# A four-layer graph network on one core: where the edge sums of layer 2 are made

## The chip, the cores and the metric

The kernel runs on one core of one Trainium2 chip. The metric is the device time of one execution in microseconds (us). The time before the change is the median of 3 runs. The profile comes from one more execution, recorded by the hardware profiler. The engines are TensorE (PE in the profile, its weight loads PEld), VectorE (DVE), ScalarE (ACT), GpSimd (POOL) and SyncE (SP). SP does nothing but issue DMA transfers in this kernel; ACT and POOL issue some as well.

## The reference, cut to what matters

There are 4096 nodes with 256 features each. `adj` is a 4096 x 4096 matrix of zeros and ones with ones on its diagonal, used by all four layers. Each layer adds its output to its input and normalizes the rows.

```python
# layer 0
agg = adj @ x / max(rowsum(adj), 1);  y = relu(concat(x, agg) @ W + b)
# layer 1, two steps n = 0, 1
R = (adj + I) / rowsum(adj + I)
A = top-p softmax of (Xa W1' W2') (Xa W3')', rows cut to mass 0.9 and renormalized
Xf = R @ Xf;  Xa = A @ Xa;  Z += Xf @ U1[n].T + Xa @ U2[n].T
# layer 2: the edge features are adj itself
nn = adj @ x
ne = einsum('ij,ji->i', adj, adj)            # the edge sums
y  = concat(x, nn, ne) @ weight + bias
# layer 3
y  = relu(normalized(adj + I) @ x @ W + b)
```

The edge sum of node i is the sum over j of adj[i, j] * adj[j, i]. It depends on `adj` alone, so it can be computed at any time before the end of layer 2.

## The kernel before

The nodes are cut into 32 tiles of 128 (`NT = 32`, `P = 128`). The host lays `adj` out twice in blocks of 128 x 128: `adjt` holds the transposed blocks that TensorE needs as weights, `adjn` the blocks of the other orientation. Both are float32 in DRAM, 2 MB for each tile of rows.

**Layer 0** runs over the 32 tiles. POOL loads `adjt` with a cast from float32 to uint8 (two DMAs per tile, L249); SP stores the bytes to the DRAM tensors `adj8_d`, which all later stages read. ScalarE casts each piece of eight blocks to the float32r format that TensorE takes (L252). The line L167 is the product of a tile row of `adj` with all node rows, each kept as an upper and a lower half, 256 + 256 columns.

**Layer 1, step 0.** While the attention logits of one tile are computed, an earlier tile is reduced to its 16 largest entries (`KEPT`), whose rows of x are gathered by POOL (`gather`, L642) and multiplied on TensorE (L733). VectorE finds maxima and their columns (`groups` L403, `tops` L498 to L502), chooses how many to keep (`pick`), and `flag` writes rows that need more work to a list in DRAM (L576, an indirect DMA of POOL). The loop of `run_step` gives each tile eight groups g of 512 columns. A group of `pieces` issues two logit products (L384), a part of the attention product, and `neighbours`: a cast of four blocks to `adjq` (L653) and four products into `acc_r` for R @ Xf (L656). In step 0 `neighbours` also makes the edge sums: POOL loads half a tile of `adjn` with a cast to uint8 (L662), ScalarE casts four blocks to float32r (L665), and TensorE multiplies the blocks of both orientations into the PSUM tile `nef_ps` (L668):

```python
for j in range(GP):
    jt = g * GP + j
    nc.tensor.matmul(pn[:, :P], a[:, j, :], b[:, j, :], start=(jt == 0),
                     stop=(jt == NT - 1))
```

In `r_end` VectorE multiplies the 128 x 128 result with the identity and sums along the rows into the column `nef[:, i]` (L682). Because `nef_ps` holds a PSUM bank, `acc_r` uses one bank in step 0 and takes turns between two banks only afterwards (`nef_done`). In `mix` the results are multiplied with U1 and U2 (L794), added up on VectorE (L796), and a key product follows (L802). The products of the first four tiles of R @ Xf run ahead of the first attention tile.

**Layer 1, step 1** has the same loop; its attention tiles are dense (L741), and its rows' normalization takes a power on POOL (`rstd`, L191). POOL has little else there: the scatter of `flag` and some gathers for tiles that were put off.

**Layer 2** runs `main` for each tile: four pieces of bytes (`a8`, five buffers, loaded by SP from `adj8_d`, L1077), ScalarE's casts (L1079), 32 products (L167) into the PSUM tile `acc`, which takes turns between two banks. `l2_end` of the tile before follows: ScalarE copies one half of `acc` (L1101), VectorE adds the other (L1102), adds the edge sum times its weight row (L1110) and the prepared rest `u` (L1111), and normalizes (L185 to L196) into `x3`, which SP stores (L1114). `l2_y` of the tile before that transposes `x3` on TensorE (L177) and multiplies it with the weights of layer 3 (L1121); VectorE splits the result into halves `yh`. The rows `x2i` and `u` are loaded by SP (L1104, L1106) and added on VectorE (L1107, L1108). **Layer 3** repeats `main` with `yh`.

Each engine runs its instructions in one fixed order. That order is not the one of the source: the framework's planner interleaves the instructions of neighbouring tiles.

Of the kernel before, what the change touches and what calls it, by code (L numbers as in the profile page):

```python
# [48 lines left out]
def gnn_stack(ctx, tc, x, adjt, adjn, w0, b0, w1, w2t, w3t, u1t, u2t, ln_g, ln_b, w2, b2, w3, b3, out):  # L49
# [12 lines left out]

    const = ctx.enter_context(tc.tile_pool(name="const", bufs=1))
# [50 lines left out]
    adj8_d = [dram.tile([P, NT, P], U8, name=f"adj8_{it}_d") for it in range(NT)]  # L114
    h_d = dram.tile([N + P, D], F32, name="h_d")
# [209 lines left out]
    with tc.tile_pool(name="l1", bufs=1, reuse_waits="tile") as l1:  # L325

        cur = {"late": False, "n": 0, "nef_done": False}
# [224 lines left out]
        def flag(st):  # L552


            pb = half("mm")
            later = st.get("later")
            if later is None:
                nc.tensor.matmul(pb[:1, 0:1], st["bad"], ones_col, start=True, stop=True)
                st["nb"] = small("nbad", 1, I32)[:1, :]
                nc.scalar.copy(st["nb"], pb[:1, :1])  # L560
                return
            nc.tensor.matmul(pb[:, 0:1], ones_sq, st["bad"], start=True, stop=True)
            nc.tensor.matmul(pb[:, 1:2], before, st["bad"], start=True, stop=True)
            sofar, slot = small("sofar"), small("slot")
            nc.vector.tensor_add(sofar, later["base"], pb[:, 0:1])

            i = st["tile"]
            at, rows_i = slots_of[cur["n"]][:, i : i + 1], ids[:, i : i + 1]
            nc.vector.scalar_tensor_tensor(slot, pb[:, 1:2], later["base"], spare, op0=ALU.add, op1=ALU.subtract)
            nc.vector.scalar_tensor_tensor(at, slot, st["bad"], spare, op0=ALU.mult, op1=ALU.add)  # L570
            later["base"] = sofar
            if i == NT - 1:

                st["to"] = to = small("to_last", 1, I32, 1)
                nc.vector.scalar_tensor_tensor(to, st["bad"], float(P), rows_i, op0=ALU.mult, op1=ALU.add)
            nc.gpsimd.indirect_dma_start(  # L576
                out=list_d[cur["n"]], out_offset=bass.IndirectOffsetOnAxis(ap=at, axis=0), in_=rows_i, in_offset=None)

# [68 lines left out]
        def neighbours(n, i, g, acc_r, pn, xf):  # L647
# [11 lines left out]
            if pn is not None:  # L659
                if g % (NLC // 2) == 0:  # L660
                    cur["b8"] = cur["w"].tile([P, NT // 2, P], U8, tag="adjn8", name="adjn8", bufs=2)
                    nc.gpsimd.dma_start(cur["b8"], adjn[i, :, g * GP : g * GP + NT // 2, :])  # L662
                b = cur["w"].tile([P, GP, P], F32R, tag="adjn", name="adjn", bufs=2)
                k = g % (NLC // 2) * GP
                nc.scalar.copy(b, cur["b8"][:, k : k + GP, :])  # L665
                for j in range(GP):
                    jt = g * GP + j
                    nc.tensor.matmul(pn[:, :P], a[:, j, :], b[:, j, :], start=(jt == 0),  # L668
                                     stop=(jt == NT - 1))

        def r_acc(i):

            return ps_acc.tile([P, 512], F32, tag=("acc", "nef")[i % 2 if cur["nef_done"] else 0], name="acc_r", bufs=1)

        def r_end(i, acc_r, pn):
# [3 lines left out]
            if pn is not None:  # L679

                junk = spare_row.bitcast(F32)[:, :P]
                nc.vector.scalar_tensor_tensor(junk, pn[:, :P], 1.0, ident, op0=ALU.mult, op1=ALU.mult,  # L682
                                               accum_out=nef[:, i : i + 1])
            nc.sync.dma_start(rows(xf_d, i), xf_new)

        def r_product(n, i, xf):

            acc_r, pn = r_acc(i), None
            if n == 0:
                pn = ps_acc.tile([P, 512], F32, tag="nef", name="nef_ps", bufs=1)  # L690
            for g in range(NLC):
                neighbours(n, i, g, acc_r, pn, xf)
            r_end(i, acc_r, pn)

        def pieces(n, st, nxt, ops, rs_now=()):
# [10 lines left out]
            if with_r:  # L706
                i, = rs_now
                acc_r, pn = r_acc(i), None
                if n == 0:
                    pn = ps_acc.tile([P, 512], F32, tag="nef", name="nef_ps", bufs=1)  # L710
# [12 lines left out]
            for g in range(NLC):  # L723
# [19 lines left out]
                if with_r:  # L743
                    neighbours(n, i, g, acc_r, pn, cur["xf"])
                for f in ops.get(g, ()):
                    f()
            if st is None:
                for i in rs_now:
                    r_product(n, i, cur["xf"])
# [6 lines left out]
            if with_r:  # L756
                r_end(i, acc_r, pn)
# [158 lines left out]
        def run_step(n, es):  # L916
# [99 lines left out]
            if n == 0:  # L1016
# [7 lines left out]
                cur["nef_done"] = True  # L1024
                for i in range(FIRST[1][0][0]):
                    r_product(1, i, cur["next"])
# [47 lines left out]
    with tc.tile_pool(name="l23", bufs=1, reuse_waits="tile") as l23:  # L1074
        def piece(it, c):
# [3 lines left out]
            nc.scalar.copy(a, a8)  # L1079
            return a  # L1080

        ahead = [piece(0, c) for c in range(NJP)]
        zh = load_halves(l23.tile([P, 4 * J0 * D], F32, name="scratch"), zu_d[:N, :], nc.sync, slice(0, D))
# [14 lines left out]

        def l2_end(it, acc):
# [7 lines left out]
            nc.vector.tensor_add(xi, xi, b2_sb)  # L1107
            nc.vector.tensor_add(u, u, xi)  # L1108
# [8 lines left out]
        def l2_y(it, x3):  # L1117
# [4 lines left out]
            y = l23.tile([P, 1, D], F32, tag="y", name="y", bufs=2)  # L1122
# [20 lines left out]
        for it in range(NT):  # L1143
            acc = main(it, lambda jt: zh[:, jt, :])
            if it > 1:
# [53 lines left out]
```

## Time and profile before

| | us |
|---|---|
| median of 3 runs (3349.98 to 3359.43) | 3354.87 |
| the profiled execution: its time | 3313.77 |
| its span, first to last instruction | 3312.0 |
| TensorE busy | 3017.6 (91%) |
| VectorE busy | 2393.5 (72%) |
| ScalarE busy | 1873.9 (57%) |
| POOL busy | 782.7 (24%) |
| edge products L668, busy | 149.4 |
| edge casts L665, busy | 159.1 |

The profiled execution took 1.2% less than the median of the runs. Busy times are sums of durations, and the durations of TensorE overlap those of their neighbours, since matmuls are pipelined; what a matmul holds up is read from start to start of neighbouring rows. In rows of the order of time, the columns are the start, the duration, the engine, the line, the operation, output and inputs, the shape, and how many instructions were merged; brackets hold the idle time ahead and what ended it. In rows of groups, the last parts are busy time and mean duration in ns of one, then the idle time ahead of the group and its releasers.

### The profile page before, as it was taken

What the parts mean: (1) busy time and instruction counts of PE and PEld (TensorE: products, weight loads), DVE (VectorE), ACT (ScalarE), POOL (GpSimd) and SP (SyncE); (2) the same over time, 40 slices, a digit from 0 to 9 for tenths busy, and PEclk for the clock granted to TensorE, in tenths of its full rate; (3) what the DMA queues carried; (4) which work ended last, traced back from release to release, by engine and by line L of the source; (5) the groups of instructions that cost most, each with busy time, mean ns of one, the idle gap of its engine ahead of it and who ended that gap; (6) DMA issues with size and microseconds to landing.
All of it is one profiled execution on the core that took longest, in us unless ns stands there. A gap on an engine that the chain in (4) does not pass through costs nothing. (4 is left out here: it accounts for less than half of the span.)

```text
span 3312.0 us, 46373 instructions
## 1 busy us (share of the span) xinstructions
PE 3017.6 (91%) x14600; PEld 2465.7 (74%) x14600; DVE 2393.5 (72%) x7121; ACT 1873.9 (57%) x3162; POOL 782.7 (24%) x916
## 2 busy tenths in 40 slices
PE   6999888999999997879989898989999787999998
PEld 5888667888888885658877777777788545888886
DVE  6888858878777776357988897888799673444444
ACT  3555666777777774455555454545455333666664
POOL 1111146666666665100000001000100001000000
PEclk9999989999999998889999999999999898999999
DMA  9988367787777776140000111011011133333332
GB/s 175 143 134 139 68 105 130 135 138 137 136 137 137 136 137 143 56 134 30 25 23 23 32 38 31 26 32 39 24 38 30 42 131 126 110 109 107 102 108 81
DMA packets 247906, 300.30 MB, mean 91 GB/s; under 512 B 34688, under 2 KB 201536, under 8 KB 247648
## 3 DMA queue, kind: packets, MB, share of 16 engines
q0 software_dynamic: 46624, 105.07, 22.8%
q1 hardware_dynamic: 188800, 180.93, 18.8%
q10 hardware_dynamic: 12224, 11.23, 1.1%
q8 instruction: 118, 1.93, 0.3%
q14 instruction: 140, 1.15, 0.1%
HBM read 331.17 MB, written 66.58 MB: 120 GB/s over the span
## 5 line engine op out<-in xcount | busy, mean ns | idle before, releaser
L656 PE MATMUL acc_r<-xh,adjq 128*128 128x512 f32 x2048 | 617.5, 433 | 22.4 <-ACT adjq L653 17.7
L741 PE MATMUL acc_bank<-xa,at 128*128 128x256 f32 x2304 | 568.8, 388 | 31.0 <-ACT at L719 30.5
L642 POOL DMA_INDIRECT G<-x_d,cols x512 | 499.4, 975 | 302.2 <-PE acc_bank L733 163.0
L167 PE MATMUL acc<-xh,a 128*128 128x512 f32 x2048 | 516.5, 405 | 17.8 <-DVE xh L144 14.0
L741 PEld LDWEIGHTS acc_bank<-xa,at 128*128 128x128 f32 x2304 | 425.3, 194 | 92.1 <-ACT at L719 41.3
L653 ACT CAST adjq<-adj 128x512 fp32r<-128x512 uint8 x512 | 316.0, 619 | 295.1 <-PE acc_r L656 97.8
L656 PEld LDWEIGHTS acc_r<-xh,adjq 128*128 128x128 f32 x2048 | 382.7, 193 | 117.6 <-ACT adjq L653 42.2
L167 PEld LDWEIGHTS acc<-xh,a 128*128 128x128 f32 x2048 | 384.6, 191 | 103.0 <-ACT xh L143 17.0
L403 DVE MAX8 cand<-e 128x8 f32<-128x256 f32 x1024 | 381.1, 414 | 93.1 <-ACT e L385 92.0
L191 POOL TENSOR_TENSOR rstd<-ve,mhalf 128x1 f32<-128x1 f32 x168 | 102.7, 611 | 1378.7 <-DVE ve L189 1338.9
L385 ACT COPY e<-lg 128x512 f32<-128x512 f32 x552 | 318.9, 584 | 176.9 <-PE lg L384 176.0
L384 PE MATMUL lg<-kS,q 128*128 128x512 f32 x1104 | 392.2, 440 | 10.7 <-ACT e L385 10.4
L1079 ACT CAST a<-a 128x1024 fp32r<-128x1024 uint8 x256 | 267.7, 1048 | 150.4 <-PE acc L167 121.7
L733 PE MATMUL acc_bank<-G,dg 128*128 128x256 f32 x1024 | 277.8, 392 | 51.5 <-DMA G<-x_d,cols 40.6
L500 DVE FIND_INDEX8 cols<-top,e 128x8 uint32<-128x4096 f32 x64 | 282.8, 4419 | 0.0
L733 PEld LDWEIGHTS acc_bank<-G,dg 128*128 128x128 f32 x1024 | 194.7, 194 | 100.7 <-DMA G<-x_d,cols 49.0
L719 ACT COPY at<-at_ps 128x512 f32<-128x512 f32 x296 | 173.5, 588 | 113.1 <-PE at_ps L716 111.6
L167 PE MATMUL acc<-yh,a 128*128 128x512 f32 x1024 | 233.7, 390 | 0.0
L252 ACT CAST a<-a 128x1024 fp32r<-128x1024 uint8 x128 | 133.5, 1048 | 157.4 <-PE acc L167 121.3
L167 PEld LDWEIGHTS acc<-yh,a 128*128 128x128 f32 x1024 | 192.2, 188 | 39.6
L384 PEld LDWEIGHTS lg<-kS,q 128*128 128x128 f32 x1104 | 182.9, 192 | 32.5 <-ACT e L385 19.4
L716 PE MATMUL at_ps<-ident,e 128*128 128x128 f32 x1184 | 183.5, 279 | 22.0 <-issue 13.8
(281 smaller groups left out, 4637.2 us busy)
## 6 DMA issues: line engine op xcount, KB each, us to landing
adj<-adj_d SPq DMA_DIRECT2D x256, 128.0 KB
a<-adj_d SPq DMA_DIRECT2D x256, 128.0 KB
a<-in_adjt POOLq DMA_DIRECT2D x64, 256.0 KB
adj_d<-a SPq DMA_DIRECT2D x64, 256.0 KB
adjn<-in_adjn POOLq DMA_DIRECT2D x64, 256.0 KB
x_d<-x SPq DMA_DIRECT2D x65, 128.0 KB
G<-x_d,cols POOLq DMA_INDIRECT x512
xf_d<-xf_new SPq DMA_DIRECT2D x64, 128.0 KB
```

The lines of the kernel that those rows point to most:

```text
L167: nc.tensor.matmul(acc, a[:, j, :], halves(jt), start=(jt == 0), stop=(jt == NT - 1))
L384: nc.tensor.matmul(pl[:, :LC], q[k], kS[:, s], start=(k == 0), stop=(k == 1))
L385: nc.scalar.copy(l[:, s], pl[:, :LC])
L403: nc.vector.max(dst[:, 8 * g : 8 * g + 8], src[:, g * GW : (g + 1) * GW])
L500: nc.vector.max_index(st["at"][:, 8 * r : 8 * r + 8], t8, st["e"][:, :N])
L642: nc.gpsimd.indirect_dma_start(out=g, out_offset=None, in_=x1_d, in_offset=bass.IndirectOffsetOnAxis(ap=st["at"][:, k : k + 1], axis=0))
L653: nc.scalar.copy(a, cur["a8"][:, g % 2 * GP : (g % 2 + 1) * GP, :])
L656: nc.tensor.matmul(acc_r, a[:, j, :], xf[:, jt, :], start=(jt == 0), stop=False)
L716: nc.tensor.transpose(ps[:, j, :], e[:, (g * G + j) * P : (g * G + j + 1) * P], ident)
L733: nc.tensor.matmul(acc_a, dg[:, k % 4, :], st["G"][k], start=(k == 0), stop=(k == KEPT - 1))
L741: nc.tensor.matmul(acc_a, ats[g][:, j, :], cur["xa"][:, jt, :], start=(jt == 0), stop=(jt == NT - 1))
L1079: nc.scalar.copy(a, a8)
```

## The change

The edge sums leave step 0. `neighbours`, `r_product` and `r_end` lose the loads, casts, products and the final multiply-and-sum, and `acc_r` takes turns between two banks in both steps. A second set of DRAM tensors, `adjn8_d`, receives `adjn` cast to uint8: in step 1, four DMAs on POOL behind each tile's list scatter, DRAM to DRAM, 512 KB read and 128 KB written by each. In layer 2 the new function `edge_sums` loads a tile's 512 KB of `adjn8_d` into a quarter of the scratch buffer (which until then holds the pieces that `zh` is split from), takes the bitwise and with the four `a8` pieces of the same tile as 32-bit integers, sums over the 32 blocks as uint16 (each holds two byte sums side by side), casts the bytes to float32, and sums over the partitions with a product of one column of ones on TensorE. The pieces `a8` therefore stay in use until VectorE has read them. The additions of `x2i` and `u` move from VectorE to POOL, and `y` has one buffer instead of two.

```diff
+    adjn8_d = [dram.tile([P, NT, P], U8, name=f"adjn8_{it}_d") for it in range(NT)]
...
-            nc.gpsimd.indirect_dma_start(
+            put = nc.gpsimd.indirect_dma_start(
                 out=list_d[cur["n"]], out_offset=bass.IndirectOffsetOnAxis(ap=at, axis=0), in_=rows_i, in_offset=None)
+            if cur["n"] > 0:
+
+                with tc.issue_after(put.ins):
+                    for c in range(NJP):
+                        s = slice(c * JP, (c + 1) * JP)
+                        nc.gpsimd.dma_start(adjn8_d[i][:, s, :], adjn[i, :, s, :])
...
-            if pn is not None:
-                if g % (NLC // 2) == 0:
-                    cur["b8"] = cur["w"].tile([P, NT // 2, P], U8, tag="adjn8", name="adjn8", bufs=2)
-                    nc.gpsimd.dma_start(cur["b8"], adjn[i, :, g * GP : g * GP + NT // 2, :])
-                b = cur["w"].tile([P, GP, P], F32R, tag="adjn", name="adjn", bufs=2)
-                k = g % (NLC // 2) * GP
-                nc.scalar.copy(b, cur["b8"][:, k : k + GP, :])
-                for j in range(GP):
-                    jt = g * GP + j
-                    nc.tensor.matmul(pn[:, :P], a[:, j, :], b[:, j, :], start=(jt == 0),
-                                     stop=(jt == NT - 1))
-
         def r_acc(i):
-
-            return ps_acc.tile([P, 512], F32, tag=("acc", "nef")[i % 2 if cur["nef_done"] else 0], name="acc_r", bufs=1)
...
+            return ps_acc.tile([P, 512], F32, tag=("acc", "nef")[i % 2], name="acc_r", bufs=1)
...
-            if pn is not None:
-
-                junk = spare_row.bitcast(F32)[:, :P]
-                nc.vector.scalar_tensor_tensor(junk, pn[:, :P], 1.0, ident, op0=ALU.mult, op1=ALU.mult,
-                                               accum_out=nef[:, i : i + 1])
...
             nc.scalar.copy(a, a8)
+            bytes_of.append(a8)
             return a
...
+        def edge_sums(it, a8s):
+
+
+            k = it % 4 * J0 * D
+            n32 = scratch[:, k : k + NT * P // 4].bitcast(I32)
+            nc.sync.dma_start(n32.bitcast(U8).rearrange("p (j i) -> p j i", i=P), adjn8_d[it])
+            W = JP * P // 4
+            for c, a8 in enumerate(a8s):
+                s = slice(c * W, (c + 1) * W)
+                nc.vector.tensor_tensor(n32[:, s], n32[:, s], a8.rearrange("p j i -> p (j i)").bitcast(I32), op=ALU.bitwise_and)
+            two = l23.tile([P, P // 2], U16, tag="two", name="two", bufs=2)
+            with nc.allow_low_precision("sums of up to 32 * 257, exact"):
+                nc.vector.tensor_reduce(two, n32.bitcast(U16).rearrange("p (j i) -> p i j", i=P // 2), axis=AX.X, op=ALU.add)
+            sums = l23.tile([P, P], F32, tag="sums", name="sums", bufs=2)
+            nc.vector.tensor_copy(sums, two.bitcast(U8))
+            ps = half("acc")
+            nc.tensor.matmul(ps[:, 0:1], sums, ones_col, start=True, stop=True)
+            nc.vector.tensor_copy(nef[:, it : it + 1], ps[:, 0:1])
...
-            nc.vector.tensor_add(xi, xi, b2_sb)
-            nc.vector.tensor_add(u, u, xi)
+            nc.gpsimd.tensor_tensor(xi, xi, b2_sb, op=ALU.add)
+            nc.gpsimd.tensor_tensor(u, u, xi, op=ALU.add)
...
-            y = l23.tile([P, 1, D], F32, tag="y", name="y", bufs=2)
+            y = l23.tile([P, 1, D], F32, tag="y", name="y", bufs=1)
...
         for it in range(NT):
             acc = main(it, lambda jt: zh[:, jt, :])
+            edge_sums(it, bytes_of[it * NJP : (it + 1) * NJP])
```

## The prediction

> **What bounds the kernel now.** I read the stages first (busy time of each engine in stretches of the span; columns PE, PEld, DVE, ACT, POOL, then granted clock, DMA share, GB/s), since the change takes work from step 0 (460 to 1274 us), adds transfers to step 1 (1440 to 2784) and VectorE work to layer 2 (2784 to 3064).
>
> ```profile
> 460.00:1274.00 814.00, 761.39 (x4005) 647.44 (x4004) 641.59 (x1875) 566.12 (x1118) 524.75 (x561) 0.99 0.75 134
> 1440.00:2784.00 1344.00, 1217.11 (x5894) 974.51 (x5893) 1080.73 (x3483) 672.91 (x1140) 108.69 (x127) 0.96 0.15 40
> 2792.00:3064.00 272.00, 269.36 (x1198) 216.15 (x1197) 123.86 (x351) 177.55 (x254) 17.01 (x31) 1.00 0.37 114
> ```
>
> TensorE bounds step 0 (94%) and layer 2 (99%); VectorE is at 79% in step 0, at 46% in layer 2. POOL and DMA have room in step 1. The chain of waits says the same of its last 560 us: TensorE's L167 alone.
>
> Then TensorE's order of time in step 0:
>
> ```profile
> 828.43 1.02 PE L733 MATMUL acc_bank<-G,dg 128*128 128x256 f32 x4
> 829.11 1.28 PE L656 MATMUL acc_r<-xh,adjq 128*128 128x512 f32 x4
> 830.23 0.56 PE L668 MATMUL nef_ps<-adjn,adjq 128*128 128x128 f32 x4
> 830.62 0.66 PE L364 MATMUL mm_bank<-xt,wq_sb 128*128 128x128 f32 x4
> ...
> 838.55 0.70 PE L733 MATMUL acc_bank<-G,dg 128*128 128x256 f32 x2 [0.74 <-DMA G<-x_d,cols]
> ...
> 845.77 0.71 PE L802 MATMUL mm_bank<-w3t_sb,xt 128*128 128x128 f32 x4 [0.58 <-DVE z L424]
> ```
>
> Ends overlap, so costs are start to start: four edge products (L668) hold TensorE from 830.23 to 830.62, 0.40 us. A tile takes 27.3 us (the flag product L562 starts at 824.59, then at 851.90). Two idles matter: one for a gather G, one for VectorE, which is late at L796 after its 4.42 us searches (L500).
>
> The removed groups and the rows that price additions:
>
> ```profile
> L665 ACT CAST adjn<-adjn 128x512 fp32r<-128x512 uint8 x256 | 159.1, 621 | 2.3 <-DMA adjn<-in_adjn 2.3
> L668 PE MATMUL nef_ps<-adjn,adjq 128*128 128x128 f32 x1024 | 149.4, 265 | 0.0
> L441 DVE TENSOR_REDUCE m_l<-e 128x1 f32<-128x4096 f32 x4 | 17.7, 4419 | 25.2 <-ACT e L385 25.2
> L435 DVE TENSOR_REDUCE m<-cand 128x1 f32<-128x128 f32 x64 | 18.1, 283 | 4.4 <-DVEq L618 2.9
> L1111 DVE TENSOR_TENSOR t<-t,u 128x256 f32<-128x256 f32 x32 | 13.6, 425 | 1.1
> ```
>
> Last, VectorE in a layer 2 tile:
>
> ```profile
> 2902.08 0.42 DVE L1102 TENSOR_TENSOR agg<-agg,acc 128x256 f32<-128x256 f32 x1 [1.64 <-ACT agg L1101]
> ...
> 2905.47 0.41 DVE L196 TENSOR_SCALAR x<-t,bn,rstd 128x256 f32<-128x256 f32 x1 [0.73 <-POOL rstd L191]
> ```
>
> From the add that empties acc to the finished x3 is 3.8 us (2902.08 to 2905.88); TensorE transposes that x3 at 2908.72. So 2.8 us of slack in a period of 8.51 us.
>
> **What the Trainium skill says.** "VectorE: DVE Perf Modes", the perf-mode tier table: tensor_reduce has one speed whatever the type, tensor_tensor in 32 bits too. The trace agrees: 4419 and 283 ns for 4096 and 128 elements are 1.04 ns each over a fixed 150 ns. "SBUF — State Buffer", Door 1: an access that crosses into a new 16-byte line pays a penalty, without saying how much. The new reduce steps 128 bytes between elements. The only strided reduce in the trace (L493: 16 elements, 32 bytes apart) has a median of 171 ns where full rate gives 169 and half rate 186: it speaks for full rate, but is too short to settle it. Same page, "Who interferes with whom": VectorE with two SBUF inputs and a GpSimd operation reading SBUF block each other; the trace before has no GpSimd adds to show it. "GPSIMD Engine Reference", 3.1: a tensor_tensor add is about 2 times VectorE's, 4497 ns for 2048 elements.
>
> **The change, part by part.**
>
> *Step 0, removed.* 1024 products, 256 casts (ScalarE, 0.62 us), 64 casting DMAs issued on POOL, 32 multiply-and-sums (VectorE, 0.36). TensorE gets back 8 x 0.40 = 3.2 us per tile. The casting DMAs share the software queue with the gathers G: one was issued at 832.28 and the gathers after it landed only at 838.5. The waits view gives TensorE 32.7 us for G between 460 and 1274; with the casts gone I credit 0.7 us per tile of it. What is late next: L802's wait for VectorE. The built program moves that product nearly one group later, but TensorE also arrives 3 us earlier. VectorE needs 12.5 us from the maxima of the last logits to L796's result (833.26 to 845.72); the wait becomes about 0.9 instead of 0.58, so 0.3 back. VectorE's 21.1 us and POOL's 17 issues of 1.25 us (21.3) fit into the new 23.7, with little room. Net 3.5 us, from 3.0 (G waits stay) to 4.3. 28 tiles run so: 98 us. The other 4 run ahead of the first tile (380 to 460), where ScalarE is busy 67.6 of 80 us: between TensorE's 32 x 0.40 = 13 us and ScalarE's 32 x 0.62 = 20; I take 15. Alternating PSUM banks for acc_r removes a wait of 1.4 us in all. Sum **-113 us** (-90 to -140).
>
> *Step 1, added.* 128 casting DMAs, DRAM to DRAM, four after each list_d scatter on POOL: 4 x 0.59 (L662's issue) = 2.4 us. POOL is idle 22.5 us between that place and the next rstd, so the issue is hidden; without that cover VectorE would wait 2.4 us for rstd. SP, TensorE and VectorE keep their order here. Transfers: a layer 0 tile moves the same bytes plus 1 MB of plain traffic in 10.3 us (L271 starts: 319.4 / 31) at a DMA share of 0.89, so four casts fill the DMA engines 9.2 us at most, of a 28.2 us tile (scatters at 1543.10 and 1571.32) whose share is now 0.08 to 0.18. Row gathers of put-off tiles queue behind the casts: five, about 1 us each, and 2 at the end. **+7** (0 to +25; no gain is possible, as nothing is removed here).
>
> *Layer 2, added.* Per tile, on VectorE: four ANDs at 0.425 (L1111's size), a reduce of 2048 elements 0.15 + 2048 x 1.04 ns = 2.29, a cast of 128x128 0.28 (L201), a column copy 0.15 (L189). Off: two adds, 0.84, to POOL. That is 3.9 + 3.6 = 7.5 us. On TensorE one column product: 0.15 to 0.2 us (L271 in layer 0). On SP one 512 KB load, 0.32 us of issue; DMA share goes from 0.37 to about 0.55. POOL's adds: an estimate from its page and rstd's 0.61 us here is 1.1 us each, after rstd and ahead of need; what they block on VectorE is between 0 and 2.2 us per tile; I take 0, because they start when their loads land, mostly beside one-input operations. The single buffer for y costs nothing while yh, which frees it, comes a whole tile ahead of the next y; if it came late, ScalarE's casts behind y would stand.
>
> The path is VectorE's latency rather than its sum. The built order puts the last AND, the reduce, the cast and the next tile's first AND between L1102 and x3 (the second AND hides in rstd's 0.73): 0.42 + 2.29 + 0.28 + 0.42 = 3.4 against 2.8 of slack. The byte pieces now wait too: the fourth piece that VectorE ANDs is loaded behind x3's store on SP. The pair before shows x3 done at 2897.37, the second load behind it landed at 2900.02: 2.65 us. From there to the next x3: AND, t, reduce, up, add, yh, statistics, cast, AND, rstd, x3, 6.8 us laid end to end, 6.5 with the overlap of neighbours. Ring 9.1 us against 8.51: 32 x 0.6 = 19. At the start, pieces of tile 1 wait for tile 0's ANDs, and these for zh's last split: about 2 us of load, 1 of cast and 1 of AND uncovered, +5 with the drain. **+24** (+8, TensorE's extra alone, to +45).
>
> Sum: -113 + 7 + 24 = **-82**. On the profiled 3313.77 us that gives 3232; the runs' median is 3354.87, 1.2% above the profiled run, and the difference is carried over: **3273**, say 3275.
>
> **Rivals.**
> 1. *The strided reduce runs at half rate*: 0.15 + 2048 x 2.08 = 4.4 us, ring 11.2, layer 2 +86 + 5. Total -113 + 7 + 91 = -15: 3340. For: the SBUF page. Against: L493's 171 ns.
> 2. *Slower*: VectorE's ring in layer 2 takes back more than step 0 gave. It decides from 8.5 + 106/32 = 11.8 us per tile. Half rate and POOL's adds in VectorE's way (2.2 us) make 13.4: 32 x 4.9 + 5 - 106 = +56, 3411. Against: VectorE has two SBUF inputs in only about a third of the time.
> 3. *Step 0 gives only part, or the casts disturb step 1*: the 21 us rings of VectorE and POOL bind at 25 us (28 x 1.2 less), or loads behind casts cost 1 us per tile (32): 3307.
> That the products stay somewhere is excluded: the built program has none.
>
> **The numbers.** Forecast 0.58, rival 1 0.25, rival 2 0.08, rival 3 0.09. A difference below 0.3% (10 us) can't be told from none. Faster: 0.58 + 0.08 + half of rival 1 (0.13) = 0.79; same: 0.08 of rival 1 and 0.01 of rival 3 = 0.09; slower 0.12. The forecast's own range is 3238 to 3305; with most of rival 1, 3238 to 3345.
>
> **What would show it.** Step 0's tiles at 23.5 to 24 us instead of 27.3, with fewer G waits; step 1's at 28.2 as now; the reduce at 2.3 us (or 4.4); layer 2's tiles at 9.1 us with TensorE idle ahead of the x3 transposes, released by VectorE. It is wrong if step 0's tile stays above 25, if step 1's grows, or if layer 2's exceeds 10.

## The result, and the profile after

The changed kernel took **3427.57 us** (median of 4 runs, 3419.87 to 3433.99) against 3352.43 for the kernel before measured beside it (4 runs): a ratio of **1.0221** (95% interval 1.0203 to 1.0238), slower. The forecast was 3275. Ratios with an interval are not quotients of the two medians, and can differ from those by up to 0.2%. The profiled execution took 3433.99 us, its span is 3432.3.

The busy time by stage, in the stretches that answer to those shown of before (us of the stretch; busy us of PE, PEld, DVE, ACT, POOL with instruction counts; granted clock, DMA share, GB/s):

```profile
460.00:1260.00 800.00, 694.92 (x3066) 556.59 (x3064) 617.82 (x1821) 450.64 (x890) 477.40 (x493) 0.94 0.53 116
1440.00:2850.00 1410.00, 1224.44 (x5885) 976.93 (x5883) 1084.31 (x3450) 669.53 (x1127) 184.53 (x261) 0.94 0.41 53
2864.00:3164.00 300.00, 257.33 (x1122) 206.04 (x1121) 227.60 (x442) 149.15 (x219) 60.00 (x83) 0.96 0.43 133
```

Step 0 has lost its 1024 products and yet is hardly shorter: TensorE is idle 13% of it, at a clock of 0.94 instead of 0.99. Step 1's DMA share has gone from 0.15 to 0.41 and the step is longer. In layer 2 TensorE, which was busy 99%, is at 86%.

Five of the waits of step 0, each with its us in total, its number and its longest (460 to 1260 us):

```profile
PE acc_r L664 <- ACT adjq L661: 24.9, 9, 6.2
ACT adjq L661 <- remote: 23.6, 7, 8.1
ACT xt L181 <- remote: 23.3, 5, 7.2
POOL G L650 <- remote: 9.8, 7, 3.7
DVE upk L203 <- remote: 7.3, 1, 7.3
```

"Remote" means that the trace holds no releaser. The first profile of the kernel before has no such wait. One of them in order of time:

```profile
563.19 0.37 ACT L181 COPY xt<-tr 128x256 f32<-128x256 f32 x1 [7.25 <-remote]
...
566.07 1.65 PE L664 MATMUL acc_r<-xh,adjq 128*128 128x512 f32 x3 [6.16 <-ACT adjq L661]
567.43 0.48 DVE L673 SCALAR_TENSOR_TENSOR xf_new<-acc_r,rs,xf_new 128x256 f32<-128x256 f32 x1 [6.69 <-ACT xf_new L672]
567.51 3.47 PE L719 MATMUL acc_bank<-G,dg 128*128 128x256 f32 x8
```

ScalarE stands still for 7.25 us, TensorE and VectorE behind it for over 6. The eight products of L719 that follow take 3.47 us; eight take 1.9 in tiles without a stop, so the clock is at half. The Trainium skill, "TensorE: Matmul & The Clock Gate", Part 1, says that the clock halves after an idle window of about 3.4 us; the trace agrees: after the stop above a clock record of 0.5 lasts 6.8 us, and most others of step 0 last 3.4 or 6.8.

In layer 2, the new groups (busy us, mean ns of one; idle time ahead of them and its releaser) and one tile of VectorE:

```profile
L1100 DVE TENSOR_REDUCE two<-scratch 128x64 uint16<-128x2048 uint16 x32 | 125.7, 3927 | 0.0
L1097 DVE TENSOR_TENSOR scratch<-scratch,a 128x256 int32<-128x256 int32 x128 | 53.3, 424 | 63.2 <-DMA a<-adj_d 62.7 <-DMA scratch<-adjn_d 0.4
L1115 POOL TENSOR_TENSOR x2i<-x2i,b_sb 128x256 f32<-128x256 f32 x32 | 25.5, 798 | 87.2 <-DMA x2i<-x_d 87.2
```

```profile
2961.28 0.41 DVE L198 TENSOR_SCALAR x<-t,bn,rstd 128x256 f32<-128x256 f32 x1 [0.44 <-POOL rstd L193]
...
2964.50 0.43 DVE L1097 TENSOR_TENSOR scratch<-scratch,a 128x256 int32<-128x256 int32 x1 [1.05 <-DMA a<-adj_d]
2964.84 0.48 DVE L1118 SCALAR_TENSOR_TENSOR t<-w2e_sb,nef,agg 128x256 f32<-128x256 f32 x1
2965.24 3.96 DVE L1100 TENSOR_REDUCE two<-scratch 128x64 uint16<-128x2048 uint16 x1
...
2969.31 0.42 DVE L1119 TENSOR_TENSOR t<-t,u 128x256 f32<-128x256 f32 x1
...
2971.79 0.41 DVE L198 TENSOR_SCALAR x<-t,bn,rstd 128x256 f32<-128x256 f32 x1 [0.44 <-POOL rstd L193]
```

From one x3 (L198) to the next are 10.5 us, and the reduce stands in the middle of that chain, between t and the add of u to it. It takes 3.93 us on the mean, not 2.29.

**Stages.** The scatters of list_d on POOL (L576 before, L578 after; 32 in a step, one per tile) cut the span well: start to the first scatter of step 0; step 0 from first to last; the gap to the first of step 1; step 1; the rest, from there to the end. Profiled executions, us:

| kernel | chip (before's median) | start | step 0 | gap | step 1 | rest | span |
|---|---|---|---|---|---|---|---|
| before, first profile | – | 430.2 | 868.6 | 174.4 | 1118.4 | 720.4 | 3312.0 |
| after, the result | 3352 | 422.3 | 861.8 | 175.6 | 1173.2 | 799.4 | 3432.3 |
| b_before | 3297 | 427.8 | 860.4 | 174.4 | 1112.1 | 719.2 | 3293.9 |
| a_after | 3297 | 420.1 | 715.9 | 173.5 | 1162.2 | 795.4 | 3267.1 |
| b_before2 | 3336 | 427.8 | 891.5 | 176.9 | 1112.0 | 722.1 | 3330.3 |
| a_after2 | 3336 | 421.8 | 860.4 | 180.5 | 1158.3 | 797.5 | 3418.5 |
| e1_drop | 3309 | 419.2 | 726.8 | 173.7 | 1111.8 | 717.0 | 3148.5 |
| e2_casts | 3309 | 419.3 | 722.8 | 174.2 | 1165.0 | 717.4 | 3198.6 |
| e3_layer2 | 3309 | 420.4 | 719.1 | 173.8 | 1111.8 | 795.6 | 3220.7 |
| e4_tree | 3309 | 419.4 | 721.4 | 174.9 | 1175.4 | 775.9 | 3267.0 |
| e5_quiet | 3297 | 420.3 | 717.1 | 173.3 | 1106.8 | 778.0 | 3195.5 |
| s0_loads | 3297 | 427.6 | 815.9 | 173.1 | 1106.1 | 721.2 | 3243.9 |
| s0_products | 3336 | 424.1 | 916.0 | 176.6 | 1104.9 | 717.3 | 3338.9 |
| e5_quiet2 | 3338 | 422.1 | 857.1 | 177.3 | 1110.2 | 770.5 | 3337.2 |
| e6_queues | 3336 | 419.2 | 855.2 | 176.5 | 1104.4 | 771.3 | 3326.6 |
| e7_order | 3338 | 421.4 | 860.6 | 178.1 | 1109.5 | 769.0 | 3338.6 |
| a_after3 | 3338 | 419.4 | 854.6 | 178.2 | 1161.2 | 796.4 | 3409.7 |
| f1_spaced | 3338 | 430.6 | 852.8 | 177.2 | 1092.2 | 794.5 | 3347.3 |
| b1_spaced | 3295 | 426.2 | 847.9 | 169.6 | 1064.4 | 724.3 | 3232.4 |
| g1_best | 3295 | 418.2 | 692.8 | 172.2 | 1060.2 | 768.1 | 3111.5 |

Each set of experiments was measured on one chip, together with the kernel before; the second column names the chip by that kernel's median. **The executions are of two sorts, and the sort goes with the chip.** On three chips (3309, 3297 and 3295) step 0 takes 693 to 727 us once its products and casts are gone; the changed kernel itself was measured on the second of them, where it is 1% faster than the kernel before. On a fourth chip (3336 and 3338 are the same one, met on two occasions) step 0 takes 853 to 861 us all the same, and the changed kernel is 2% slower. The result, with 3352 for the kernel before, is like the fourth; which chip it is from is not known. "First sort" and "second sort" mean these below; the second was studied on one chip alone. Between a_after and a_after2, the same program, step 0 differs by 144 us, the gap by 7, and the rest by 4 or less each.

### The profile page after: what moved, and what is told of

Its sections match the earlier page's. It is cut to its first block, busy times and chain, and to the rows that moved or that the text cites. A ratio compares the mean times of both kernels' runs of the same rounds, so it can differ in the third digit from the quotient of the medians.

```text
span 3432.3 us, 44427 instructions
## 1 busy us (share of the span) xinstructions
PE 2973.3 (87%) x13640; PEld 2382.5 (69%) x13640; DVE 2517.5 (73%) x7217; ACT 1741.6 (51%) x2906; POOL 864.3 (25%) x1044
## 5 line engine op out<-in xcount | busy, mean ns | idle before, releaser
L664 PE MATMUL acc_r<-xh,adjq 128*128 128x512 f32 x2048 | 621.5, 434 | 65.6 <-ACT adjq L661 51.0
L169 PE MATMUL acc<-xh,a 128*128 128x512 f32 x2048 | 532.2, 413 | 19.6 <-DVE xh L146 18.4
L664 PEld LDWEIGHTS acc_r<-xh,adjq 128*128 128x128 f32 x2048 | 385.3, 195 | 172.0 <-ACT adjq L661 83.6
L169 PEld LDWEIGHTS acc<-xh,a 128*128 128x128 f32 x2048 | 394.7, 196 | 110.2 <-ACT xh L145 20.2
L719 PE MATMUL acc_bank<-G,dg 128*128 128x256 f32 x1024 | 289.0, 406 | 35.7 <-DMA G<-x_d,cols 16.3
L719 PEld LDWEIGHTS acc_bank<-G,dg 128*128 128x128 f32 x1024 | 201.0, 202 | 85.5 <-issue 19.3
L386 PEld LDWEIGHTS lg<-kS,q 128*128 128x128 f32 x1104 | 195.4, 194 | 74.2 <-ACT e L387 27.0
L705 ACT COPY at<-at_ps 128x512 f32<-128x512 f32 x296 | 173.7, 589 | 114.3 <-PE at_ps L702 112.8
L702 PE MATMUL at_ps<-ident,e 128*128 128x128 f32 x1184 | 183.6, 279 | 23.4 <-issue 15.2
```

Of the source, the lines that this page charges most:

```text
L169: nc.tensor.matmul(acc, a[:, j, :], halves(jt), start=(jt == 0), stop=(jt == NT - 1))
L386: nc.tensor.matmul(pl[:, :LC], q[k], kS[:, s], start=(k == 0), stop=(k == 1))
L664: nc.tensor.matmul(acc_r, a[:, j, :], xf[:, jt, :], start=(jt == 0), stop=False)
L702: nc.tensor.transpose(ps[:, j, :], e[:, (g * G + j) * P : (g * G + j + 1) * P], ident)
L719: nc.tensor.matmul(acc_a, dg[:, k % 4, :], st["G"][k], start=(k == 0), stop=(k == KEPT - 1))
```

## Experiments

**Three parts alone, and a faster reduce.** Four kernels on one chip, with the kernel before at 3308.53. The first is the changed kernel without its additions:

```diff
-            if cur["n"] > 0:
-                with tc.issue_after(put.ins):
-                    for c in range(NJP):
-                        s = slice(c * JP, (c + 1) * JP)
-                        nc.gpsimd.dma_start(adjn8_d[i][:, s, :], adjn[i, :, s, :])
+    nc.vector.memset(nef, 0.0)
-            edge_sums(it, bytes_of[it * NJP : (it + 1) * NJP])
```

> The changed kernel without its additions: no casting transfers in step 1, no edge sums in layer 2 (the edge counts are set to zero, so this part of the computation is left out). What stays of the change is the removal in step 0 and the two adds on POOL. Theory A (the stages add up; step 0 gives only what the changed kernel's trace shows, about 15 us with its earlier start, because VectorE's and POOL's chains per tile take over from TensorE): about 3340 us, step 0's flags still 27 us apart on average. Theory B (the forecast's step 0 is right by itself and something in the changed kernel's run disturbed it): about 3240 us, step 0's tiles at 23.5 to 24 us.

Measured: 3149.13, ratio 0.9513 (0.9495 to 0.9531). Step 0 alone is worth more than the forecast said, not less: theory A falls; the tiles are shorter than B has them. Step 0's tiles take 22.4 us in the second half, where the forecast had 23.5 to 24.

> The same with the casting transfers of step 1 put back; their bytes are read by nothing, and the edge sums of layer 2 are still left out. Theory A (row gathers of the put-off tiles stand behind the casts in the software queue): 55 to 65 us more than without the casts, all of it between the first and the last list scatter of step 1 and the 17 us after it, in tiles that have a put-off row under way. Theory B (the casts are hidden and step 1 grew for another reason, a lower clock for instance): less than 15 us more.

Measured: 3210.86, 62 us more by the medians; the profiled spans differ by 50, with 53 more in step 1. A's amount is right. Its tiles are too: 41.4 to 49.1 us in the first, 37.1 to 41.6, 36.7 to 43.3 and others where put-off rows are under way, none in the seven tiles of 28.2 us in between. The waits of step 1, first without and then with the casts, show who is late:

```profile
ACT adjq L656 <- DMA adj<-adj_d: 24.1, 6, 5.7
DVE from_l L843 <- DMA to_l<-list_d: 16.5, 3, 6.5
```

```profile
ACT adjq L662 <- DMA adj<-adj_d: 51.4, 8, 9.2
DVE from_l L849 <- DMA to_l<-list_d: 31.2, 3, 10.6
```

The adjacency loads of SP's own queue lose 27 us, the reads of the put-off list 15. It is not only gathers behind casts in one queue.

> The changed kernel without the casting transfers of step 1; layer 2's edge sums read the first adjacency copy instead of the second, the same bytes in number, so the counts are those of the wrong matrix and the work is the same. Theory A (the strided reduce at half rate makes VectorE's ring 10 us per tile): 45 to 55 us more than without edge sums, layer 2 at about 320 us. Theory B (layer 2 was slowed by the clock or by what was left of step 1): under 25 us more.

Measured: 3229.77, 81 us more than e1_drop, 79 of them after step 1. Layer 2's tile is as long as in the result, without any cast in step 1. A is the nearer one and too low in its sum: from one tile's `t` to the next are 10.5 us on the mean of 31 intervals instead of 8.2, which is 71 us, and the first `t` comes 8 us later.

For the fourth, the reduce becomes a tree:

```diff
-                nc.vector.tensor_reduce(two, n32.bitcast(U16).rearrange("p (j i) -> p i j", i=P // 2), axis=AX.X, op=ALU.add)
+                n16, k = n32.bitcast(U16), NT * P // 4
+                while k > P // 2:
+                    nc.vector.tensor_tensor(n16[:, :k], n16[:, :k], n16[:, k : 2 * k], op=ALU.add)
+                    k //= 2
+                nc.vector.tensor_tensor(two, n16[:, :k], n16[:, k : 2 * k], op=ALU.add)
```

> The changed kernel with one edit: the strided reduce of 2048 uint16 is replaced by five contiguous uint16 adds of 1024, 512, 256, 128 and 64 elements, with the same sums. Theory A (the stride halves the rate, and the reduce sets layer 2's tile): five adds of 0.15 us fixed and 1984 elements take 2.8 us at 1.04 ns per element and 1.8 us at half of that, against 3.95; the tile falls by 1.1 to 2.1 us, the whole by 35 to 48 us, to 3380 to 3392. Theory B (POOL's adds in VectorE's way, or the late loads of the byte pieces set the tile): under 15 us less.

```profile
L1102 DVE TENSOR_TENSOR scratch<-scratch 128x1024 uint16<-128x1024 uint16 x32 | 21.2, 663 | 0.0
L1102 DVE TENSOR_TENSOR scratch<-scratch 128x512 uint16<-128x512 uint16 x32 | 13.2, 412 | 0.1
L1102 DVE TENSOR_TENSOR scratch<-scratch 128x256 uint16<-128x256 uint16 x32 | 9.3, 291 | 1.0
L1102 DVE TENSOR_TENSOR scratch<-scratch 128x128 uint16<-128x128 uint16 x32 | 8.1, 253 | 1.0
```

With the last add of 215 ns that is 1.83 us in place of 3.93. The strided reduce ran at 1.85 ns per element ((3927 - 150) / 2048), little more than half the rate of the contiguous one of float32 (1.04). That the stride is the reason, and not the 16-bit type, is argued and not shown: no contiguous uint16 reduce was run. The mean tile only falls from 10.5 to 9.9 us and the last stage by 20 us. 3266.35 is 0.9867 (0.9850 to 0.9883) of the kernel before, a_after on its chip 0.9904: some 12 us, little more than the two intervals leave open. On the tile A is wrong and B right: the ANDs' waits for byte pieces grew from 58 to 86 us in all.

**The same program on other chips.**

> The changed kernel again, beside its parts' chip if the same one comes up. Theory A (the parts add: the removal alone 3149, casting transfers +62, layer 2 +80, and the 862 us of step 0 in the first profile, with its waits that the trace puts down to 'remote', belong to that execution): about 3291 us, 0.995 of the kernel before, step 0's flags 722 us from first to last. Theory B (what the parts alone don't show comes from having them together): 1.022 of the kernel before, step 0 again near 862 us.

Measured: 3266.75, ratio **0.9904** (0.9886 to 0.9921). A holds in the main: the parts sum to 0.9948, a little above the interval, and step 0 is 716 us.

> The kernel before, for a profile beside the others. Theory A: step 0's tiles at 27.3 us as in the first profile of it, 869 us from the first flag to the last. Theory B (the chip matters to this kernel too): tiles above 27.3 us where the changed kernel's are above 22.4.

One run, 3295.59; tiles of 27.3 us as in the first profile. TensorE's order in step 0 of a_after answers to the one shown of before:

```profile
802.55 1.02 PE L719 MATMUL acc_bank<-G,dg 128*128 128x256 f32 x4
803.22 1.27 PE L664 MATMUL acc_r<-xh,adjq 128*128 128x512 f32 x4
804.33 0.38 PE L179 MATMUL tr<-ident,xf 128*128 128x128 f32 x2
...
810.01 1.28 PE L664 MATMUL acc_r<-xh,adjq 128*128 128x512 f32 x4
811.13 0.39 PE L386 MATMUL lg<-kS,q 128*128 128x512 f32 x1
811.46 0.71 PE L788 MATMUL mm_bank<-w3t_sb,xt 128*128 128x128 f32 x4
```

After an L664 group comes the next work 1.1 us later and without a wait, and the product that stood 0.58 us for VectorE (L802, now L788) doesn't stand any more.

> The changed kernel a third time. Theory A (the first measurement of it met something on its chip that two other chips don't have): 0.985 to 0.996 of the kernel before again on a chip where that kernel takes about 3300 us; on one where it takes 3350 us, 1.02 and the waits called 'remote' again in step 0. Theory B (the first measurement was a single disturbed sitting): 0.985 to 0.996 whatever the kernel before takes.

> The kernel before, for a profile on the same chip as the run above. If that chip gives 3350 us for it, Theory A expects the excess over 3300 us in step 0, with waits put down to 'remote' or to nothing; if it gives 3300 us, step 0's tiles at 27.3 us.

On this chip the kernel before took 3336.16 (29 runs) and the changed one 3409.75, ratio **1.0198** (1.0173 to 1.0222), with step 0 at 860 us. The kernel before lost 31 us in its own step 0 too (b_before2 against b_before) and has 34 us of waits called "remote" in it. Theory A holds: the loss comes with the chip, 144 us for the changed kernel and 31 for the kernel before.

> The changed kernel again, on the chip of the three runs above. If the kernel before takes about 3300 us here: 0.985 to 0.996 of it, step 0 near 720 us. If it takes 3335 to 3355 us: 1.015 to 1.025 of it, step 0 near 860 us, with most of the semaphore events of step 0 missing in its trace.

The same chip again: 3408.37, ratio 1.0190 (1.0161 to 1.0220). As expected.

**Step 0: products or loads.** Into e1_drop only the loads and casts go back:

```diff
+                if g % (NLC // 2) == 0:
+                    cur["b8"] = cur["w"].tile([P, NT // 2, P], U8, tag="adjn8", name="adjn8", bufs=2)
+                    nc.gpsimd.dma_start(cur["b8"], adjn[i, :, g * GP : g * GP + NT // 2, :])
+                b = cur["w"].tile([P, GP, P], F32R, tag="adjn", name="adjn", bufs=2)
+                k = g % (NLC // 2) * GP
+                nc.scalar.copy(b, cur["b8"][:, k : k + GP, :])
```

is s0_loads; s0_products takes the same lines from the kernel before and puts `b = a` in their place.

> The kernel with the removal alone, and step 0's adjacency transfers into SBUF and ScalarE's casts of them put back; the products and the sums of the edge counts stay left out (the counts are zero). Theory A (the gain of step 0 is TensorE's products, and the transfers cost it only the waits for G): 20 us or less above 3149. Theory B (ScalarE's casts and the transfers are half of the 147 us that step 0 gave): 60 to 80 us above it.

> The kernel before with one edit: step 0's transfers of the second adjacency copy and ScalarE's casts of them are gone, and its edge products read the first copy on both sides, so the counts are those of another matrix and TensorE's work is the same. The run with the products away and the loads kept gave only 42 us of the 150. Theory A (products and loads are two limits of almost the same height: with either in place the other's removal gives little): 10 to 40 us below the kernel before, tiles of 26 to 27 us set by TensorE. Theory B (the two add up): about 105 us below it.

s0_loads took 3255.39, ratio 0.9882 (0.9860 to 0.9903); the removal of both was 0.9513, so the loads and casts as they stand in this program cost 3.7%, some 120 us. The profiled spans differ by 95 us, 89 of them in step 0 and 8 ahead of it. From 480 to 800 us ScalarE waits for the loads:

```profile
ACT adjn L668 <- DMA adjn<-in_adjn: 61.9, 18, 7.6
```

Later the tiles take 22.3 us, as with the loads gone. The casts by stretch (busy time and number of ScalarE's casts, granted clock, DMA share, GB/s) say why, first in s0_loads (L668), then in b_before (L665):

```profile
480.00:800.00 320.00, 84.00 (x144) 0.94 0.82 141
960.00:1220.00 260.00, 0.00 (x0) 1.00 0.62 142
```

```profile
480.00:800.00 320.00, 54.09 (x87) 0.98 0.74 133
```

The loads and casts do not stand where they stood. Nothing reads the cast blocks any more, and in the built program they run ahead: 10 to 15 casts in each of the first 18 tiles, where the kernel before has 8 in most tiles to the end, then none. This run puts neither theory to the test at the old places. s0_products fell on a chip of the second sort: 3339.51, 1.000 (0.9987 to 1.0013) of the kernel before, with tiles of 29.3 us; it says nothing certain of the first sort. What the pair leaves: on the first sort, products gone with the loads and casts moved forward gave 45 us of step 0 (860 to 816), both gone gave 134 to 145. How the 134 to 145 divide between products and loads is not shown.

**Where the casts stand.** e4_tree with the casts of 21 tiles after scatters 1 to 7, three tiles' each, the rest one each at 11 later ones:

```diff
-                    for c in range(NJP):
-                        s = slice(c * JP, (c + 1) * JP)
-                        nc.gpsimd.dma_start(adjn8_d[i][:, s, :], adjn[i, :, s, :])
+                    for k in CASTS.get(i, ()):
+                        for c in range(NJP):
+                            s = slice(c * JP, (c + 1) * JP)
+                            nc.gpsimd.dma_start(adjn8_d[k][:, s, :], adjn[k, :, s, :])
```

> The changed kernel with the tree of contiguous adds, and with the casting transfers of step 1 moved: those of 21 tiles are issued after the scatters 1 to 7, three tiles' after each, where no put-off row is under way, and those of the other 11 one each after scatters 10, 14, 17, 18, 22 and 25 to 30, whose tiles did not grow. The bytes moved are the same. Theory A (the cost of the casts is row gathers and list scatters that stand behind them in the software queue): step 1 falls from 1175 us to about 1120, the whole by 45 to 55 us against the tree alone. Theory B (the casts cost bandwidth wherever they are): under 15 us less, the first tiles above 28.2 us.

Measured: 3197.68, ratio **0.9690** (0.9670 to 0.9709). Step 1 is 1106.8, below the kernel before; the quiet tiles stay at 28.2 to 28.3 us with three times the bytes. A holds, and is exceeded (step 1 is 69 us below e4_tree's, on another chip): the casts cost by their place, not by their bytes.

> The kernel with the tree and the moved casts again, for a comparison with the run above on the same chip. If the kernel before takes about 3300 us here: 0.969 of it, as before. If it takes 3335 to 3355 us: step 0 near 855 us instead of 717, and 0.992 to 1.0 of the kernel before.

On the second sort: 3334.96, 0.9989 (0.9966 to 1.0012), step 0 at 857. As expected.

**Layer 2's order.** Two more edits on e5_quiet: u's load and x3's store on POOL's queue, then the edge sums after the end of the tile before.

```diff
-            nc.sync.dma_start(u, rows(zu_d, it)[:, D:])
+            nc.gpsimd.dma_start(u, rows(zu_d, it)[:, D:])
-            nc.sync.dma_start(rows(x3_d, it), x3)
+            nc.gpsimd.dma_start(rows(x3_d, it), x3)
```

> The changed kernel with the tree of adds and the moved casts, and one more edit in layer 2: the load of u and the store of x3 are issued on POOL's queue instead of SP's. On SP both stand ahead of the next tile's byte pieces, and wait for VectorE (4.8 and 2.6 us a tile in the profile), so VectorE's ANDs wait for pieces that were issued late. Theory A (this queue order, not VectorE's work, sets layer 2's tile of 10.0 us): 8.6 to 9.2 us per tile, 25 to 45 us less than without the edit. Theory B (VectorE's chain sets it): under 10 us less.

> The kernel with the tree, the moved casts and the two transfers on POOL's queue, and one more edit in layer 2: the edge sums of a tile come after the end of the tile before it in program order, so that the add of u to t stands ahead of the next tile's first AND on VectorE. In the profile without this edit the AND waits 2.9 us a tile for its byte piece, with t, the statistics and x3 behind it; the piece is late because its load stands on SP behind a buffer that POOL frees only after the x3 of the tile before: a ring through VectorE's order. Theory A (this ring sets the 9.9 us): 8.6 to 9.3 us per tile, 20 to 40 us less than with the edge sums first. Theory B (VectorE's total of work sets it): under 8 us less.

Both on the second sort: 3326.98, 0.9962 (0.9941 to 0.9983), and 3327.18, 0.9963 (0.9951 to 0.9975). The tile is 9.90 and 9.80 us: both miss theory A. In e6_queues the ANDs still wait for their pieces; SP's loads of x2i wait for a buffer that POOL's add of u frees (68 us in 27 waits), ahead of the pieces. e7_order didn't put its order to the test: the built program keeps an AND ahead of the add of u in the steady tiles.

```profile
2951.74 0.43 DVE L1099 TENSOR_TENSOR scratch<-scratch,a 128x256 int32<-128x256 int32 x1 [2.51 <-DMA a<-adj_d]
2952.08 0.42 DVE L1125 TENSOR_TENSOR t<-t,u 128x256 f32<-128x256 f32 x1
```

So the ring through x3, POOL's add, SP's order and the byte piece is read from these lines; that it sets the 9.8 us has not been shown.

**The list scatter.** Each list_d scatter writes 128 rows of 4 bytes side by side. In a_after one is issued at 795.81; the DMA view from 792 to 832 (slices of 1 us) shows what follows:

```profile
GB/s 232 114 94 111 175 100 0 107 31 101 111 67 108 333 289 224 315 152 131 53 211 229 162 66 131 139 101 170 0 115 29 78 26 42 33 52 200 354 327 380
```

In the seven slices from 798 to 805 all queues together move 0 to 111 GB/s, then 333; the next scatter does the same from 820. f1_spaced and the two after it put the rows 64 bytes apart:

```diff
-    list_d = [dram.tile([N + P, 1], I32, name=f"list{n}_d") for n in range(STEPS)]
+    list_d = [dram.tile([16 * (N + P), 1], I32, name=f"list{n}_d") for n in range(STEPS)]
...
+            nc.vector.tensor_scalar(at16, at, 16.0, None, op0=ALU.mult)
```

> The changed kernel with the rows of the put-off list 64 bytes apart in DRAM instead of 4 (the index is multiplied by 16 in one more VectorE operation of 0.15 us). After each scatter of 128 rows of 4 bytes the trace of all runs shows both queues at 40 to 60 KB per us for 8 us, and then 300. Theory A (neighbouring 4-byte writes block each other, and the adjacency loads and gathers behind them): the low stretch is under 4 us, step 1 falls by 10 us or more, and on a chip where step 0 takes 860 us it falls toward 720. Theory B (128 writes of this kind take that long wherever they land): the low stretch stays at 8 us and no stage changes by more than 5 us beyond the scatter of a repeat.

Measured, second sort: 3348.96, 1.0032 (1.0020 to 1.0043) against 1.0190 for the changed kernel beside it. Over the 8 us from 2 us after a scatter the rate is 104 GB/s instead of 58 (mean of step 0's 32 scatters in f1_spaced and a_after3). Single packets show what stood still: among those of 4096 bytes in step 0, one in a hundred took over 3.1 us in a_after3 and over 0.58 us in f1_spaced, at the same median of 0.16; the longest of 1024 bytes took 7.9 and 0.7. Step 1 falls by 69 us, from 1161 in a_after3 to 1092: A holds for step 1. Step 0 stays at 853: A fails there, and the scatter is not what the second sort of chip does to step 0. The 4-byte fill of the wider list costs the start 11 us.

> The kernel with the tree, the moved casts, the two transfers on POOL's queue and the edge sums after the end of the tile before, and with the put-off list's rows 64 bytes apart as well; the list is now filled from an SBUF tile in whole rows, so the 10 us that the 4-byte fill cost layer 0 in the run before are not spent. Theory A (the scatters hold up step 1 with the casts moved too): step 1 falls from 1110 us to about 1090, the whole by 15 to 25 us: about 0.990 of the kernel before where that takes 3335 us or more, 0.96 where it takes 3300. Theory B (the scatters only cost together with casts after each of them): under 6 us.

> The kernel before with one edit, the same spacing of the put-off list. Theory A: step 1 falls from 1112 us to about 1095, the whole by 15 to 25 us, about 0.994; step 0 the same within 5 us on a chip where it is limited by TensorE. Theory B (no cost without the casts): the ratio is 1.0 within 0.2%.

First sort: b1_spaced 3233.51, **0.9813** (0.9797 to 0.9829); g1_best, with all edits, 3110.82, **0.9441** (0.9425 to 0.9457). Both gained more than theory A said: step 1 falls by 48 us from b_before to b1_spaced and by 47 from e5_quiet to g1_best, and step 0 by 12 and 24 us. g1_best's row over the same 40 us, with its scatter at 793.98, has two low slices where there were seven:

```profile
GB/s 98 148 246 17 25 196 175 242 190 112 111 120 298 180 94 102 131 127 180 170 234 137 127 74 193 4 131 103 175 145 211 119 74 247 190 253 151 78 131 103
```

g1_best was not measured on the second sort; e7_order, the same without the spacing, is 0.9963 there.

## Why the prediction was wrong

The sum was -113 + 7 + 24 = -82. On a chip of the first sort it came out as -152 + 50 + 76 and -1 in the gap, -27 (a_after against b_before); on the second as -37 + 46 + 75 and +4, +88 (a_after2 against b_before2). Two terms were too small on every chip. The first was too small on one sort and three times too large on the other.

*Step 0, "net 3.5 us, 28 tiles run so, 98 us".* On the first sort the main mechanism was right: TensorE bounds the step, tiles fall from 27.3 to 22.4 us. The size was low. Between 600 and 1100 us of b_before, start to start, the edge products held TensorE 69.3 us in 18.3 tiles, 3.8 us a tile instead of 3.2: one group in eight is split in two by other work (36 pairs beside 128 whole groups) and then holds it 1.05 us instead of 0.39, and one group read off the trace doesn't show that. TensorE's waits (480 to 1120) fell from 32 us in 23.4 tiles to 14 in 28.6, 0.9 us a tile, where 0.7 was credited for G and 0.3 taken back for L802. The size is near and the reason was wrong: the waits for G stayed (7.2 us there, 10.8 after), while those at L802 (10.2 us) and for ScalarE's `xt` (10.4 us) went. 3.8 and 0.9 make 4.7 of the 4.9.

Of the casting loads, the prediction counted only the waits for G. Whether they and ScalarE's casts would have been the next limit at the faster pace is not shown, as s0_loads moved them. They went together with the products, so the sum doesn't depend on it.

On the second sort, which is that of the result, this term gave 37 us instead of 113, and the step that failed is the one ahead of the sum: that the profiled execution stands for the chip that is timed. The first profile was 1.2% below the median of the runs. The prediction carried this over as a factor. In b_before2 against b_before 31 of the 36 us are in step 0, the very stage that the change bets on, and the first profile has the tiles of the first sort, no "remote" wait and nearly all completion events (below). Which chip it ran on isn't known.

*Step 1, "row gathers queue behind the casts: five, about 1 us each; +7".* The issues were hidden, as said: POOL's casts (L585, 0.53 us each) delay nobody by themselves, and quiet tiles stay at 28.2. The bound of 9.2 us of transfers was fair: in e5_quiet's first tiles twelve casts land within 26 us of the first issue, 8.7 for four. What failed is the list of those who wait: not five gathers of 1 us, but above all adjacency loads (27 us more) and list reads (15 more), in a step that is 50 us longer. In part this is so because the casts came right behind a scatter that had already slowed the queues for 8 us; not wholly, as step 1 with the spaced list is still 1092 us with the casts there (f1_spaced) and 1064 without any (b1_spaced, on another chip). Spacing the list took 69 us from the changed kernel's step 1, moving the casts 55, and spacing alone took 48 from a step without casts.

*Layer 2, "a reduce of 2048 elements 2.29 us; ring 9.1".* The ring was right and the reduce wrong: 9.1 plus the 1.64 us that it took longer is 10.7; the middle tiles of a_after take 10.7, those of the result 10.9. That the ring is what sets them was tested only in part: with a reduce of 1.83 us the middle tiles still take 10.2 (e4_tree), where the ring's sum would have about 8.6; the ANDs' waits for byte pieces grew instead. Rival 1 (0.25) had the rate nearly right, at 2.08 ns per element, and a ring of 11.2. The evidence that decided against it, L493 with 16 elements of 4 bytes 32 bytes apart, was called too short and followed all the same; and by the prediction's own 150 ns and 1.04 ns it has 167 at full rate and 183 at half rate, not 169 and 186, so that 171 spoke for full rate less clearly. The Trainium skill, "SBUF — State Buffer", Door 1, has a penalty for every new 16-byte line; if it is that penalty, its size here is 0.8 ns per element at 128 bytes between elements (1.85 against 1.04). The other prices held: AND 0.424 (0.425), cast 0.22 (0.28), copy 0.15 (0.15); POOL's adds took 0.80 and 0.78 instead of 1.1.

*Rivals.* Rival 2 (slower, ring over 11.8) has the sign of the result and not its mechanism. Rival 3 named two of the result's causes, "step 0 gives only part, or the casts disturb step 1", at 1 us a tile; the first came to 4 us a tile on the second sort, and the second to 1.6.

**Open:** what the second sort of chip does to step 0. Instruction durations are as short there (of the 84 groups in a_after and a_after2, 500 to 1100 us, the medians of 80 agree within 2%, and the other four are longer in a_after), and packets of 4096 bytes take 159 ns at the median on both. A stop of one engine for 3 to 8 us holds up the others, and the halved clock after it adds up to 46 us (59.2 us of clock time lost in step 0 against 13.0). It is neither the reduce, the casts nor the scatter, as e5_quiet2, e6_queues and f1_spaced have step 0 at 853 to 857 us there. One trait sets these traces apart. A trace holds one completion event for nearly every packet of 4 bytes, but between 460 and 1120 us a_after2 has 2799 for 9824, the result 2985 for 9740 and b_before2 3798 for 10240, against 11890 for 11993 in a_after and 10508 for 10568 in the first profile of before; in layer 0 and step 1 a_after2 and a_after hold the same share, within 1%. Whether late or lost semaphore events are the cause or a mark of it can't be told from these runs, nor whether the chip itself matters or something that goes with it. The waits called "remote" may be waits for transfers whose event is missing.

## What to carry to other kernels

A profile that is a per cent off its own timed runs may be of another chip: find the stage that holds the difference before betting on that stage. A transfer is not priced by its bytes but by what stands behind it in every queue at that place; moving the casts to quiet tiles made them free, and the scatter of 4-byte rows, which no one had listed as a cost, was worth 1.9% by itself. When a price rests on one short strided instruction, take the slower rate until a longer one is seen. And when an experiment takes away what reads a result, count per stretch where the rest still stands: without their reader, s0_loads' casts moved into other tiles.

## What the hardware showed that was not expected

- After an indirect scatter of 128 neighbouring 4-byte rows to DRAM all queues together move 47 to 65 GB/s for 8 us (means of step 0's 32 scatters in b_before, a_after3 and a_after); with the rows 64 bytes apart it is 104 to 135 (f1_spaced, b1_spaced, g1_best), and the kernel before gains 1.9%. Single packets of 1024 bytes took up to 5 to 8 us in step 0 before, and up to 1.2 us after.
- The same program differs by 4.4% between two chips (3267 and 3410 us) where another differs by 1.2% (3297 and 3336), nearly all of it in one stage.
- A uint16 reduce with 128 bytes between its elements runs at 1.85 ns per element; contiguous uint16 adds run at 0.49 ((663 - 412) / 512), float32 adds at 1.04 ((691 - 425) / 256, L263 and L266 of e4_tree).
